# An edge-gated graph layer: another order of the first two groups, and earlier edge lists

## The chip, the core and the metric

The kernel runs on one core of a Trainium2 chip. The metric is the device time of one execution in microseconds (us). The kernel before took 1029.48 us in the median of three runs (1023.50, 1029.48 and 1036.24).

## What is computed

There are 16 graphs (batches) over the same 1024 nodes, with 256 features each. The adjacency matrix is sparse: an entry exists with a chance of about 0.8% and on the diagonal, so a node has some nine edges. The reference, cut to what matters:

```python
pre_u = einsum('bud,dk->buk', h, W1[:d]);  pre_v = einsum('bvd,dk->bvk', h, W1[d:])
hidden = relu(pre_u[:, :, None, :] + pre_v[:, None, :, :] + b1)
S   = sigmoid(einsum('buvk,ko->buvo', hidden, W2)[..., 0] + b2[0])
a_t = einsum('buv,bud->bvd', S * A, h)
m_t = einsum('uv,bud->bvd', A, h) * h
z   = beta1 * h + beta2 * (a_t @ Wa + ba) + beta3 * (m_t @ Wm + bm)
```

Taken densely, `hidden` would have 16 x 1024 x 1024 x 256 elements. Since S is multiplied by A, only the pairs with an edge count, and the kernel computes only those.

## The kernel before

**Groups, blocks, steps.** The 16 batches are four groups g of four (GB = 4). The 1024 target nodes are eight tiles vt of 128 (NT = 8). A pair (g, vt) is a block; there are 32, and `order` (lines 376 to 379) says in which order they run. A block has T = 10 steps: two halves of 64 targets, by five chunks of 128 edge slots. So a step handles up to 128 edges for four batches, and step n belongs to block n // 10.

**One step.** GpSimd (POOL) issues an indirect DMA (line 513) that fetches, for each of the 128 slots, one row of 8 KB from `table[g]` in HBM into one of eight buffers `fetched`. The row is pre_u and h of the source node for four batches. TensorE (PE) multiplies a 0/1 matrix `mark` with X, the target's pre_v with its bias (line 622), into `pc`; VectorE (DVE) adds `pc` to the row (line 652, called the add below) and takes relu and the dot product with W2 for each of four batches (line 659, the gate); ScalarE (ACT) applies the sigmoid (662) and scales the left operand (630, 666); PE sums the weighted rows h of the edges into `acc` (675). The buffer is then free, and POOL issues the fetch of step n + 8 into it.

**Once per block.** `halves` makes X of the next block from `hT`, the tile of h with the features on the partitions (pieces at the steps s = 0, 2, 5, 6, 7 of a block); `turn_over` and `block_end` transpose the sums, multiply by Wa and Wm and store z (pieces at s = 4 to 7, line 746; line 714 is VectorE's part of it).

**The tables.** `table[g]` has to stand before the first fetch of group g, eight steps ahead of that group's first block. For each of its eight tiles, `rows` computes pre_u in two halves (four matmuls by w_u on line 411 each, an ACT copy `tab`, and a DMA to the table, line 439), and `copy_h` sends h from HBM to HBM (405). `plan` (lines 806 to 814) sets the steps of the halves for groups 1 to 3. `load_hT` (400) loads the tile h that `rows` and `halves` need, in pieces of 512 bytes; a block of group 0 has it in the tile `wide` already. Places for it are few, so the tiles in `again` are dropped after their rows and loaded a second time.

**The lists.** `lists(vt)` (236 to 346) makes the edge list of one target tile for all groups: a key load from the adjacency (238), VectorE work to find and order the entries (245 to 300), three ACT operations for `mark` (305 to 307), a cast, four DMAs and five matmuls that spread it (309 to 316), and VectorE work for the row numbers `uidx` that the fetches need (323 to 344). Its values come by ten small indirect DMAs on POOL (353, `val`), one or two a step, behind a fetch. Lists 0 to 3 are made before the first step; 4 to 7 run beside the steps: `start_list` (803) names the step at which each begins. `lists` is a generator. At a yield of "op" it gives way until the next place between two gate pieces (`fill` on 658, four places a step); "load", "wait", "slot" and "step" make it pause for some steps (642).

**Queues.** Every engine runs its instructions in the order in which this code issues them. SP's queue issues nearly all plain DMAs, POOL's all indirect ones.

## Time and profile before

| | |
|---|---|
| three runs, us | 1036.24, 1029.48, 1023.50 |
| the profiled execution, us | 1026.43 |
| its span from the first to the last instruction, us | 1024.6 |
| mean granted TensorE clock | 0.984 |
| busy: PE, DVE, ACT, POOL, us | 957.0, 948.3, 889.0, 438.2 |
| moved by DMA | 375.00 MB, mean 366 GB/s |
| first add (line 652) starts at, us | 60.4 |

The profile is one execution. Where this document speaks of block k, it means the stretch from the start of the first add of block k to that of block k + 1; the windows of the trace are cut there. The windows give the busy time of each engine, the granted share of TensorE's clock (PEclk), the busy share of the 16 DMA engines and the rate. Busy minus length is idle time of that engine.

### The profile page before, as it was taken

Reading aid. Unit: us, or ns where it says so; the run is one execution under the profiler, and the core shown is the slowest. Engines: PE = TensorE matmul, PEld = TensorE weight load, DVE = VectorE, ACT = ScalarE, POOL = GpSimd, SP = SyncE. Lnnn points to the kernel's source line nnn. Section 1 sums busy time; section 2 is a strip of 40 time slices with the busy share of each in tenths; the row PEclk is TensorE's granted clock in tenths of the full one; section 3 lists DMA queues with packets and bytes.
Section 4 is the critical chain, followed back from the end, with each engine's and each line's share of the span. In section 5 each row is a group of like instructions: output and inputs, shape, how many; then the busy total and the mean of one; then the engine's idle time right before and its main releaser. Section 6 shows DMA issues by size and latency. Waiting matters only on the chain.

```text
span 1024.6 us, 21644 instructions
## 1 busy us (share of the span) xinstructions
PE 957.0 (93%) x6408; PEld 696.9 (68%) x6408; DVE 948.3 (93%) x3302; ACT 889.0 (87%) x2754; POOL 438.2 (43%) x441
## 2 busy tenths in 40 slices
PE   7877989998899999999999999999999999999996
PEld 5744766665566766776677777777777666677663
DVE  7588969879998999998999999999999999999994
ACT  3666978978898999888999999999999999999984
POOL 3166656555337332563343333434333434444430
PEclk9988999999999999999999999999999999999998
DMA  9899999999899999999999999999999999999992
GB/s 329 300 356 383 376 340 322 351 364 343 301 342 343 396 412 387 343 365 381 411 414 411 411 406 405 412 393 414 383 413 394 383 375 365 365 370 368 377 369 70
DMA packets 128702, 375.00 MB, mean 366 GB/s; under 512 B 17616, under 2 KB 83152, under 8 KB 92368
## 3 DMA queue, kind: packets, MB, share of 16 engines
q0 software_dynamic: 48640, 296.70, 74.3%
q1 hardware_dynamic: 79312, 76.30, 22.4%
q8 instruction: 53, 0.87, 0.3%
q10 hardware_dynamic: 624, 0.52, 0.2%
q14 instruction: 73, 0.60, 0.2%
HBM read 377.53 MB, written 50.33 MB: 418 GB/s over the span
## 4 chain that ended last, share of the span: by engine, by line
PE 56%; DVE 23%; ACT 8%; issue 8%; DMA 3%; POOL 1%; another core or an unknown queue 0%; POOLq 0%; DVEq 0%
PE misc L411 16%; DVE fetched L659 11%; PE misc L746 11%; PE pc L622 10%; PE acc L675 9%; DVE fetched L652 8%; PE misc L697 4%; DMA fetched<-table,uidx 3%; ACT left L666 2%; PE misc L730 1%; DVE LT L714 1%; PE misc L415 1%; ACT ev L683 1%; ACT X L906 1%; POOL fetched L513 1%
## 5 line engine op out<-in xcount | busy, mean ns | idle before, releaser
L513 POOL DMA_INDIRECT fetched<-table,uidx x320 | 342.7, 1071 | 501.3 <-PE acc L675 353.8
L659 DVE SCALAR_TENSOR_TENSOR fetched<-fetched,w_b 128x256 f32<-128x256 f32 x1280 | 472.3, 416 | 0.0
L652 DVE TENSOR_TENSOR fetched<-fetched,pc 128x1024 f32<-128x1024 f32 x320 | 387.6, 1211 | 28.9 <-PE pc L622 10.2
L666 ACT ACTIVATE left<-left,gt 128x16 f32<-128x16 f32 x1280 | 285.8, 299 | 0.0
L622 PE MATMUL pc<-X,mark 128*128 128x512 f32 x640 | 229.8, 451 | 20.7 <-DVE fetched L652 11.9
L675 PE MATMUL acc<-fetched,left 128*32 128x256 f32 x2560 | 183.6, 388 | 4.6 <-ACT ev L683 3.1
L622 PEld LDWEIGHTS pc<-X,mark 128*128 128x128 f32 x640 | 105.0, 189 | 109.8 <-issue 59.3
L675 PEld LDWEIGHTS acc<-fetched,left 128*32 128x32 f32 x2560 | 71.8, 109 | 81.9 <-issue 23.2
L662 ACT ACTIVATE gt<-sc,b_b 128x4 f32<-128x4 f32 x320 | 96.8, 303 | 30.4 <-DVE fetched L659 22.0
L746 PE MATMUL misc<-w_a,LT 128*128 128x256 f32 x496 | 117.4, 379 | 0.7 <-ACT LT L424 0.7
L746 PE MATMUL misc<-w_m,LT 128*128 128x256 f32 x496 | 117.3, 379 | 0.0
L746 PEld LDWEIGHTS misc<-w_a,LT 128*128 128x128 f32 x496 | 93.6, 189 | 15.6 <-ACT LT L424 1.5
L630 ACT ACTIVATE left<-onehot,val 128x32 f32<-128x32 bf16 x320 | 100.1, 313 | 0.0
L411 PE MATMUL misc<-w_u,wide 128*128 128x256 f32 x384 | 92.0, 388 | 8.0 <-DMA w_u<-in_W_dram 7.3
L353 POOL DMA_INDIRECT val<-in_adjT_dram,vidx x80 | 85.0, 1063 | 33.8 <-issue 22.8
L659 DVE DVE_READ_ACCUMULATOR fetched<-fetched,w_b 128x1 f32 x1280 | 99.0, 77 | 0.0
L683 ACT COPY ev<-acc 128x512 f32<-128x512 f32 x160 | 92.3, 577 | 6.8 <-PE acc L675 2.3
L746 PEld LDWEIGHTS misc<-w_m,LT 128*128 128x128 f32 x496 | 89.5, 190 | 9.8
L697 PE MATMUL misc<-ident,ev 128*128 128x128 f32 x642 | 83.9, 275 | 11.7 <-ACT ev L683 5.8
L411 PE MATMUL misc<-w_v,wide 128*128 128x256 f32 x368 | 91.5, 394 | 0.0
L697 PEld LDWEIGHTS misc<-ident,ev 128*128 128x128 f32 x642 | 74.5, 142 | 22.4 <-ACT ev L683 6.6
L411 PEld LDWEIGHTS misc<-w_u,wide 128*128 128x128 f32 x384 | 73.6, 194 | 21.1 <-DMA w_u<-in_W_dram 7.3
(160 smaller groups left out, 980.2 us busy)
## 6 DMA issues: line engine op xcount, KB each, us to landing
table<-in_x_dram SPq DMA_DIRECT2D x32, 512.0 KB
out_dram<-z SPq DMA_DIRECT2D x62, 256.0 KB
table<-tab SPq DMA_DIRECT2D x48, 256.0 KB
wide<-in_xT_dram SPq DMA_DIRECT2D x18, 512.0 KB
fetched<-table,uidx POOLq DMA_INDIRECT x320
hT<-in_xT_dram SPq DMA_DIRECT2D x10, 512.0 KB
wide<-in_xT_dram SPq DMA_DIRECT2D x4, 1024.0 KB
table<-fetched SPq DMA_DIRECT2D x8, 512.0 KB
```

The lines of the kernel that those rows point to most:

```text
L411: nc.tensor.matmul(p[:, bb * D:(bb + 1) * D], hT[:, 2 * h + bb, i, :], wt[:, i, :], start=(i == 0 and not begun), stop=(i == DC - 1), skip ...
L513: nc.gpsimd.indirect_dma_start(out=fetched[at_slot[n]], out_offset=None, in_=table[g], in_offset=bass.IndirectOffsetOnAxis(ap=uidx[:, vt * ...
L622: nc.tensor.matmul(pcs[n][:, c], marks[n // TW][:, j * P:(j + 1) * P], cuts[k][w][:, c], start=True, stop=True)
L630: nc.scalar.activation(lefts[n][:, 1::GB, :], onehot[:, vt * NW + w, j, :].unsqueeze(1).to_broadcast([P, GB // 2, V]), AF.Copy, scale=val[ ...
L652: nc.vector.tensor_tensor(t, t, pcs.pop(n), ALU.add)
L659: nc.vector.scalar_tensor_tensor(t[:, b, :], t[:, b, :], 0.0, w2_b, ALU.max, ALU.mult, accum_out=sc[:, b:b + 1])
L662: nc.scalar.activation(gt, sc, AF.Sigmoid, bias=b2_b)
L666: nc.scalar.activation(lefts[n][:, 2 * b, :], lefts[n][:, 1 + b // 2 * GB, :], AF.Copy, scale=gt[:, b:b + 1])
L675: nc.tensor.matmul(accs[i][b * 2 * V:(b + 1) * 2 * V, r, :], left[:, 2 * b - b % 2:2 * b - b % 2 + 2].rearrange("p k v -> p (k v)"), f[:, ...
L683: nc.scalar.copy(evs[i], accs.pop(i))
L697: nc.tensor.matmul(pt[:, :, FROM[j]:FROM[j] + V], evs[i][:, r, c * P:(c + 1) * P], ident, is_transpose=True, start=(j == of[0]), stop=True ...
L746: nc.tensor.matmul(pz[:, bb * D:(bb + 1) * D], LT[:, 2 * h + bb, i if bb else 1 - i, c, :], wt[:, c, :], start=(i == 1 and bb == 0 and c = ...
```

## The change

Five things change together.

1. **Order.** Group 0 runs all its eight blocks first, then group 1, 2 and 3. Before, the order was (0, tiles 0 to 5), (1, tiles 0 to 5), then tiles 6 and 7 of group 0 and of group 1. So the first block of group 1 is block 8 and not block 6, and two tiles are loaded a second time and not four; those loads are due 20 steps ahead of their block and not 9.
2. **Table 1.** Its rows are made in pairs of steps from (4, 6) to (61, 63), about one tile per block; before, from (4, 6) to (39, 41), two tiles per block.
3. **Lists.** Lists 4 to 7 start at steps 6, 12, 25 and 38, before at 7, 14, 44 and 82. They wait five steps for their key and not eight. `LISTS`, the step at which their memory goes to three more places for h, is 70 and not 110.
4. **Products.** After the three ACT operations a list now pauses two steps before its matmuls ("pause"), before one ("step").
5. **Key.** At step 0, list 4's key load is issued ahead of a load of h.

```diff
@@ lists
         nc.scalar.activation(mark, mark, AF.Relu)
-        yield "step"
+        yield "pause"
         nc.scalar.copy(few, mark)
@@ order
-    FIRST = 6
-    order = [(g, vt) for some in (range(FIRST), range(FIRST, NT)) for g in range(2) for vt in some]
-    again = [(g, vt) for g in range(2) for vt in range(FIRST, NT)]
-    order += [(g, vt) for g in range(2, NG) for vt in range(NT)]
+    TWICE = 2
+    order = [(g, vt) for g in range(NG) for vt in range(NT)]
+    again = [(1, vt) for vt in range(NT - TWICE, NT)]
@@
-    ROOM, MORE, LISTS, AHEAD = 10, 3, 110, 14
+    ROOM, MORE, LISTS, AHEAD = 10, 3, 70, 14
@@
-    turn = [(g, vt) for g in range(2) for vt in (*range(FIRST, NT), *range(FIRST))]
+    turn = [(g, vt) for g in range(2) for vt in (*range(NT - TWICE, NT), *range(NT - TWICE))]
@@ piece_of
-            r[1:] = said not in ("slot", "step"), n + {"load": 8, "wait": 2, "slot": 1, "step": 1}.get(said, 0)
+            r[1:] = (said not in ("slot", "step", "pause"),
+                     n + {"load": 5, "wait": 2, "slot": 1, "step": 1, "pause": 2}.get(said, 0))
@@
-    start_list = dict(zip((7, 14, 44, 82), range(EARLY, NT)))
+    start_list = dict(zip((6, 12, 25, 38), range(EARLY, NT)))
@@ plan
-    plan(turn[NT:], ((4, 6), (9, 11), (13, 18), (19, 21), (23, 28), (29, 31), (33, 38), (39, 41)))
+    plan(turn[NT:], ((4, 6), (9, 13), (19, 23), (29, 33), (39, 43), (49, 53), (58, 59), (61, 63)))
@@
-    pending.extend((order.index(k) * T - T + 1, k) for k in again)
+    pending.extend((order.index(k) * T - 2 * T, k) for k in again)
@@ step 0
             for i in advance[0]:
                 next(made[i], None)
+            next(made[EARLY])
             load_hT(turn[NT + 1])
-            next(made[EARLY])
```

No instruction of the list or of a block is added or removed; the program has two loads of h fewer (line 400). Three places show how the order moves. In the rows, `misc` and `pc` are accumulators, `w_u` and `w_v` the halves of W1, `hT` and `wide` the tiles of h; in the changed kernel lines 376 to about 640 have one number less.

First, TensorE at steps 40 to 43 (block 4), where `pc<-X,mark` is the product of a step. Before:

```order
L622 MATMUL pc<-X,mark 128x512 x2
L411 MATMUL misc<-w_u,wide 128x256 x4
L622 MATMUL pc<-X,mark 128x512 x2
L415 MATMUL misc<-b_p,unit 128x512
L411 MATMUL misc<-w_v,wide 128x256 x4
L675 MATMUL acc<-fetched_188,left 32x256 x4
L675 MATMUL acc<-fetched_189,left 32x256 x4
L622 MATMUL pc<-X,mark 128x512 x2
L411 MATMUL misc<-w_u,wide 128x256 x4
L622 MATMUL pc<-X,mark 128x512 x2
L415 MATMUL misc<-b_p,unit 128x512
L411 MATMUL misc<-w_v,wide 128x256 x4
```

and in the changed kernel:

```order
L621 MATMUL pc<-X,mark 128x512 x2
L410 MATMUL misc<-w_u,wide 128x256 x4
L621 MATMUL pc<-X,mark 128x512 x2
L414 MATMUL misc<-b_p,unit 128x512
L410 MATMUL misc<-w_v,wide 128x256 x4
L675 MATMUL acc<-fetched_188,left 32x256 x4
L675 MATMUL acc<-fetched_189,left 32x256 x4
L621 MATMUL pc<-X,mark 128x512 x4
L414 MATMUL misc<-b_p,unit 128x512
L410 MATMUL misc<-w_v,wide 128x256 x4
```

The second half of a table row (w_u) between the two halves of X (w_v) is gone from here.

Second, VectorE at the adds of steps 31 to 33 (block 3), where `fetched<-fetched,pc` is the add, `fetched,sc` the gate pieces and `key` and `cand` belong to a list. Before:

```order
L652 TENSOR_TENSOR fetched_189<-fetched_189,pc 128x1024
L659 SCALAR_TENSOR_TENSOR fetched_188,sc<-fetched_188,w_b 128x256 x4
L714 TENSOR_TENSOR LT<-LT,wide 128x2x4x64
L652 TENSOR_TENSOR fetched_182<-fetched_182,pc 128x1024
L659 SCALAR_TENSOR_TENSOR fetched_189,sc<-fetched_189,w_b 128x256 x4
L652 TENSOR_TENSOR fetched_183<-fetched_183,pc 128x1024
```

and in the changed kernel:

```order
L652 TENSOR_TENSOR fetched_189<-fetched_189,pc 128x1024
L245 SCALAR_TENSOR_TENSOR key<-key,ukey 128x512
L659 SCALAR_TENSOR_TENSOR fetched_188,sc<-fetched_188,w_b 128x256
L245 SCALAR_TENSOR_TENSOR key<-key,ukey 128x512
L659 SCALAR_TENSOR_TENSOR fetched_188,sc<-fetched_188,w_b 128x256 x3
L714 TENSOR_TENSOR LT<-LT,wide 128x2x4x64
L652 TENSOR_TENSOR fetched_182<-fetched_182,pc 128x1024
L254 MAX cand<-key 128x8
L659 SCALAR_TENSOR_TENSOR fetched_189,sc<-fetched_189,w_b 128x256
L254 MAX cand<-key 128x8
```

List 6 stands here now, which before was issued between steps 53 and 68; list 7, before between the adds of steps 91 and 106, is now issued between those of steps 44 and 63.

Third, SP's queue at step 0. Before:

```order
L312 DMA whose<-few 64x640 x4
L400 DMA wide<-in_xT_dram 128x8x128
L238 DMA key<-in_adjT_dram 128x1024
L96 DMA w_a<-in_Wa_dram 128x2x256
L96 DMA w_m<-in_Wm_dram 128x2x256
```

and in the changed kernel:

```order
L312 DMA whose<-few 64x640 x4
L238 DMA key<-in_adjT_dram 128x1024
L399 DMA hT_204<-in_xT_dram 128x8x128
L96 DMA w_a<-in_Wa_dram 128x2x256
L96 DMA w_m<-in_Wm_dram 128x2x256
```

List 4's key changes places with a load of h, and VectorE's first operation on it (line 245) stands one step earlier, after the add of step 7 and not of step 8.

## The prediction, as it was put on record

> **What bounds the kernel now.** I read the page's totals first, then the windows cut at each tenth add (line 652), then who waited for whom, then the chain of waits inside the longest blocks. The page:
>
> ```profile
> PE 957.0 (93%) x6408; PEld 696.9 (68%) x6408; DVE 948.3 (93%) x3302; ACT 889.0 (87%) x2754; POOL 438.2 (43%) x441
> ```
>
> PE and DVE are both busy 93% of the span, so the shares name no bound; they are an average over stages. So I cut the trace by block. Each row is one block, 0 to 12; the last two rows are blocks 13 to 22 and 23 to 30.
>
> ```profile
> 60.40:95.50 35.10, 25.12 (x125) 16.02 (x126) 28.59 (x95) 20.58 (x66) 23.01 (x22) 0.79 1.04 389
> 95.50:128.70 33.20, 32.50 (x206) 24.29 (x204) 31.34 (x122) 28.92 (x88) 21.79 (x22) 0.97 1.05 376
> 128.70:170.40 41.70, 36.49 (x222) 26.04 (x222) 33.24 (x123) 32.44 (x94) 25.93 (x25) 0.96 0.95 326
> 170.40:204.20 33.80, 31.65 (x212) 23.58 (x213) 30.20 (x111) 28.45 (x85) 19.02 (x18) 1.00 1.02 350
> 204.20:240.30 36.10, 33.52 (x220) 23.74 (x223) 28.35 (x95) 28.67 (x92) 19.98 (x20) 1.00 0.95 344
> 240.30:272.20 31.90, 27.42 (x177) 18.11 (x169) 31.59 (x114) 27.58 (x85) 11.38 (x11) 1.00 0.94 346
> 272.20:303.30 31.10, 28.68 (x209) 20.09 (x209) 29.94 (x110) 28.70 (x88) 11.46 (x10) 1.00 0.90 326
> 303.30:335.00 31.70, 29.65 (x203) 21.02 (x195) 27.92 (x94) 26.70 (x85) 22.13 (x21) 1.00 0.96 338
> 335.00:362.60 27.60, 27.39 (x178) 20.39 (x178) 27.60 (x96) 26.16 (x85) 10.73 (x10) 1.00 1.02 401
> 362.60:394.50 31.90, 30.05 (x212) 21.60 (x214) 31.90 (x120) 28.28 (x87) 10.68 (x10) 1.00 1.02 396
> 394.50:425.50 31.00, 29.66 (x190) 22.12 (x183) 29.65 (x107) 29.61 (x90) 11.35 (x11) 0.94 1.02 371
> 425.50:457.30 31.80, 30.98 (x215) 22.08 (x216) 28.15 (x94) 27.13 (x85) 21.35 (x20) 1.00 1.00 356
> 457.30:489.20 31.90, 30.06 (x208) 21.47 (x200) 27.86 (x93) 27.41 (x86) 11.89 (x12) 1.00 1.03 386
> 489.20:767.50 278.30, 277.61 (x1916) 208.89 (x1916) 277.07 (x936) 266.63 (x840) 104.13 (x99) 1.00 1.03 407
> 767.50:979.80 212.30, 206.28 (x1450) 148.79 (x1448) 211.68 (x739) 202.25 (x666) 86.39 (x80) 1.00 0.98 375
> ```
>
> The columns after the length are PE, its weight loads, DVE, ACT, POOL, then clock, DMA share, GB/s. From block 13 on DVE does not pause: 277.07 of 278.30, or 27.7 us a block, and 211.68 of 212.30 after that. There the change moves nothing. In blocks 1 to 12 DVE is idle 36.0 us (length less busy, row by row): 1.86, 8.46, 3.60, 7.75 in blocks 1 to 4; 0.31 and 1.16 in 5 and 6; 3.78 in 7; none in 8 and 9; 1.35 in 10; 3.65 and 4.04 in 11 and 12. **So the measure of this change is DVE's idle time:** DVE executes the same instructions in both kernels, and the time changes by as much as that idle time does. Blocks 9 and 10, in which list 7 runs, show what a list costs: 61.55 busy, against 55.4 for two plain blocks, 6.2 us.
>
> Who made DVE wait (all of the run):
>
> ```profile
> DVE LT L714 <- ACT LT L424: 13.8, 9, 3.3
> DVE fetched L652 <- PE pc L622: 10.2, 13, 2.4
> DVE fetched L652 <- PE acc L675: 9.9, 4, 4.9
> DVE fetched L652 <- DMA fetched<-table,uidx: 4.9, 5, 3.9
> ```
>
> Mostly PE, or ACT behind PE; a late fetch, 4.9 us in all. The chain of waits in block 4 says what PE was doing:
>
> ```profile
> 209.24 1.73 PE misc L411 x8
> ...
> 211.66 1.73 PE misc L411 x8
> ...
> 215.05 1.73 PE misc L411 x8
> ...
> 217.48 1.73 PE misc L411 x8
> ```
>
> Four half tiles of pre_u and pre_v (each eight records of 1.73 us together) within 10 us, in three steps. The ACT copies `tab` count the pre_u halves per block (the last number before the clock; blocks 1 to 5 and 7):
>
> ```profile
> 95.50:128.70 33.20, 1.78 (x3) 0.97 1.05 376
> 128.70:170.40 41.70, 2.35 (x4) 0.96 0.95 326
> 170.40:204.20 33.80, 2.33 (x4) 1.00 1.02 350
> 204.20:240.30 36.10, 1.74 (x3) 1.00 0.95 344
> 240.30:272.20 31.90, 0.00 (x0) 1.00 0.94 346
> 303.30:335.00 31.70, 1.18 (x2) 1.00 0.96 338
> ```
>
> DVE idles where there are three or four, and hardly where there are none, even beside a list.
>
> **The change part by part**, as DVE idle time taken or added.
>
> *Table 1 in pairs, one tile a block.* Blocks 1 to 5 get two halves each, as blocks 7 to 22 have, and list work in each (list 4 to 7, 6.2 us each, spread over steps 7 to 63). Idle there: 21.7 us in blocks 1 to 4. The nearest rows with a list and at most two halves are blocks 5, 9 and 10: 0.31, 0 and 1.35, mean 0.55. Four such blocks keep 2.2 us. Block 2 ran at a clock of 0.96, which is 1.7 us of PE time; I leave that in, since nothing in the edit excludes it. So 21.7 - 2.2 - 1.7 = 17.8 us go. Bounds: nothing goes, or all 21.7. The cover is DVE's own list work, which makes each step longer; if it is gone (a list that has ended), PE's 29.7 us of block 10 still lies under DVE's.
>
> *The two tiles at (58, 59) and (61, 63)* put four halves into steps 58 to 63, most in block 6. Blocks 2 and 3 had four: 8.46 and 3.60 idle, the first with a slow clock and two lists. I take block 3, so 3.6 against 1.16 now: +2.4 us. Bounds 0 and +7.3.
>
> *Lists 6 and 7 earlier.* The DVE work moves from blocks 5, 6, 9 and 10 to 3 to 6: no change of the sum. What moves with it is the values, `val` on POOL:
>
> ```profile
> 95.50:128.70 33.20, 12.14 (x12) 0.97 1.05 376
> 303.30:335.00 31.70, 10.43 (x10) 1.00 0.96 338
> 425.50:457.30 31.80, 9.85 (x9) 1.00 1.00 356
> ```
>
> Blocks 7 and 11 hold ten and nine of them and no list; beside the fetches POOL is busy 22.13 and 21.35 us there, against 10.7 in a plain block, and DVE idles 3.78 and 3.65. Block 1 has twelve beside a list and three table halves, and idles 1.86. In the changed kernel list 6's values stand beside list 7, list 7's own after it, in blocks 6 and 7. I take one of the two phases off, -3.7 us; that the values are the cause is read from where they stand, not shown. Bounds 0 and -7.4.
>
> *List 4's key ahead of h.*
>
> ```profile
> 72.12 0.53 SPq L400 DMA_DIRECT2D wide<-in_xT_dram  x1
> 72.69 2.67 SPq L238 DMA_DIRECT2D key<-in_adjT_dram  x1
> 91.74 0.69 DVE L245 SCALAR_TENSOR_TENSOR key<-key,ukey 128x512 f32<-128x512 f32 x1 [4.72 <-DMA key<-in_adjT_dram]
> ```
>
> The key took 19.0 us from issue to use, and DVE stood 4.72 us at the head of its queue. The key now goes one load earlier, but is needed a step (an add and a gate, about 2.8 us) earlier too. One load of 512 KB at block 0's 389 GB/s is 1.3 us; so I leave the wait, 0. Bounds -4.7 and +2.
>
> *The other keys* have five steps and not eight. Blocks 1 to 4 last 144.8 us, 3.6 us a step, so 18.1 us. Behind a DVE that waits for a key stand the gate, hence ACT's sigmoid, PE's sum and POOL's next fetch. The only row that shows a key late is the one above, with 19.0 us: 0.9 us each, +2 us, with shorter steps counted. Bounds 0 and +6.
>
> *SP's queue.* With a tile of table 1 move its load of h, its copy of h and its two stores, by the shapes 0.5 MB for the load, the copy and the pair of stores each. Blocks 1 to 4 make 14 halves now and 8 in the changed kernel, so three tiles, about 4.7 MB of the 50.3 MB that pass there, go to blocks 5 and 6; with each list go its key and four small stores. Fewer stores that wait for a `tab` stand ahead of the keys. DVE waited for fetches only 4.9 us in the whole run, so I take 0.
>
> *Two loads of h fewer*, 1 MB of 375: at 407 GB/s 2.6 us of transfers, beside DVE's work. 0, bound -2.6. *Products two steps behind*: PE's wait for `made` lies inside blocks that are counted already, 0. *Table 1 due at step 72*: its last rows are made at step 63, nine steps ahead; table 2 and 3 have eight (rows to 144, fetch at 152), and blocks 15 and 16 show no idle for it. 0.
>
> Block 12's 4.04 us stay: step 120 is the same in both.
>
> Sum: -17.8 + 2.4 - 3.7 + 2 = **-17 us**, so the profiled execution's 1026.4 us would be 1009.3. That execution lies 3 us under the median of the three runs, so on the median's scale it is 1012; between these I put 1010. Its own range is 997 to 1021: below, the better ends of the first and third term with the second and the keys at 0 (-29); above, a third of the first term lost and the keys at +6.
>
> **The rivals.**
>
> *Transfers bind.* If blocks 1 to 6 are slow because small loads and stores keep the DMA engines at the 338 GB/s that blocks 2 to 6 show on average, then their 71.5 MB (length by rate, row by row) take 211 us however the work is spread; they take 207.8 now. Only the values' 3.7 us and the two loads' 2.6 are gained: 1020. For it: the DMA share is 0.90 to 1.05 in every row. Against it: the share is 1.03 in blocks 13 to 22 too, at 407 GB/s, where DVE does not wait; and a late fetch cost 4.9 us in all. At 407 GB/s the 71.5 MB take 176 us, less than DVE's 190.8 us of work there (184.7 in the six rows and list 7's 6.2). The Trainium skill (DMA: Bandwidth & Descriptors, Where 436 GB/s comes from) puts the limit between HBM and one core at about 358 GB/s and the ports' at 435; by 358 those bytes would take 200 us, and the gain in blocks 1 to 6 would be 8 us, an estimate of 1015. The 407 GB/s over 278 us in the rows above is over that limit, so I go by the row.
>
> *List operations hold up the gate.* One mechanism on DVE: up to four list operations stand between the four pieces of a gate, so the sigmoid, the sum on PE and the fetch eight steps ahead all come later, and DVE then waits for what it delayed itself. If block 2's 8.46 us is its price and not that of PE's halves, blocks 1 to 5 idle 42.3 us where they now idle 22.0: +20.3 in place of -17.8, and with the other terms (+0.7) 1047. It is slower than before from 4.3 us a block on. For it: block 2 holds parts of lists 4 and 5. Against it: blocks 5 and 9 hold list work (31.59 and 31.90 busy) and idle 0.31 and 0.
>
> *Everything evens out.* If the first key comes in time and blocks 6, 7 and 11 become plain too, all idle time but block 12's and a clock window goes: 36.0 - 4.0 - 1.7 + 4.7 = 35, so 991.
>
> *The edit does not do what it says*: rows that now stand at s = 3 could collide with the next block's pieces, and the idle time of blocks 1 to 4 stays. Then only the values count: 1023.
>
> **How the numbers follow.** Forecast 0.66, of which a little over half lies below 1008.9; transfers 0.17; list operations hold up the gate 0.05; everything evens out 0.05; no effect 0.07. A measurement of this kernel tells about 2%, 20.6 us, from no change: faster than 1008.9 is 0.36 of the forecast and the 0.05, 0.41; slower than 1050.1 is the upper part of the slower rival, 0.03; 0.56 lies between. The range leaves out the slower rival and half of the fastest: 996 to 1026.
>
> **What would show it.** Right: blocks 1 to 4 at 32 to 35 us each with DVE idle under 1.5; two `tab` copies per block; blocks 8 to 11 at 28 us with no list; block 6 at 33 with PE ahead of DVE's wait. Wrong: blocks 1 to 4 still with 3 us or more of idle beside two copies (then it was not PE's halves); a rate of 340 GB/s with late fetches (transfers); a wait of several us on `key` in lists 5 to 7; POOL waiting at the first fetch of table 1.

## The result, and the profile after

The changed kernel takes 1021.1 us in the median of 19 runs, the kernel before 1028.7 us on the same chip: a ratio of 0.994, with an interval of 0.9918 to 0.9962. So it is faster by 6 us. The medians count all runs; the ratio leaves out two of the changed kernel's that fell into a slower state. The forecast was 17 us on the profiled execution; the two profiled executions differ by 5.8. Its profiled execution spans 1018.7 us, that of before 1024.6.

The page's totals show that DVE does the same work as before, as the prediction assumed; its idle time fell by 5.8 us, and so did the span.

```profile
PE 956.9 (94%) x6408; PEld 703.8 (69%) x6408; DVE 948.2 (93%) x3302; ACT 888.6 (87%) x2754; POOL 439.0 (43%) x441
```

The windows of the changed kernel, cut at each tenth add (now line 652 as before; lines 376 to 640 count one less). One row per block, 0 to 12, then blocks 13 to 22. Columns: length, PE, its weight loads, DVE, ACT, POOL, clock, DMA share, GB/s.

```profile
59.90:93.80 33.90, 25.23 (x125) 16.10 (x126) 28.90 (x95) 20.62 (x66) 23.34 (x22) 0.81 1.04 383
93.80:130.30 36.50, 32.40 (x212) 23.16 (x211) 32.55 (x122) 27.81 (x87) 26.21 (x24) 0.99 1.01 373
130.30:165.30 35.00, 31.68 (x192) 23.50 (x191) 32.52 (x124) 30.92 (x91) 20.59 (x21) 0.95 0.88 296
165.30:203.30 38.00, 34.32 (x206) 24.90 (x203) 33.52 (x128) 31.12 (x93) 23.51 (x22) 0.91 0.91 319
203.30:238.50 35.20, 32.29 (x225) 23.21 (x225) 32.61 (x121) 31.11 (x92) 19.43 (x18) 1.00 0.95 341
238.50:271.70 33.20, 29.12 (x178) 21.14 (x175) 30.05 (x114) 27.18 (x83) 21.73 (x20) 0.95 0.94 340
271.70:308.90 37.20, 36.89 (x249) 28.14 (x247) 29.45 (x101) 31.00 (x96) 17.24 (x17) 0.95 0.93 336
308.90:338.80 29.90, 28.55 (x186) 20.69 (x188) 28.04 (x95) 26.00 (x84) 15.58 (x14) 1.00 1.03 394
338.80:366.30 27.50, 27.50 (x193) 20.68 (x185) 27.50 (x96) 26.36 (x85) 10.66 (x10) 1.00 1.03 414
366.30:393.80 27.50, 27.50 (x192) 20.63 (x191) 27.50 (x94) 26.58 (x85) 10.96 (x10) 1.00 1.03 410
393.80:421.50 27.70, 27.70 (x194) 20.83 (x193) 27.70 (x96) 26.93 (x85) 10.52 (x10) 1.00 1.03 407
421.50:449.40 27.90, 27.90 (x196) 21.02 (x195) 27.72 (x94) 26.79 (x85) 10.50 (x10) 1.00 1.03 409
449.40:483.30 33.90, 31.61 (x221) 22.82 (x219) 27.95 (x97) 28.26 (x87) 11.39 (x12) 0.96 1.02 376
483.30:761.60 278.30, 278.08 (x1916) 209.45 (x1917) 277.29 (x932) 266.41 (x839) 104.97 (x100) 1.00 1.02 404
```

Blocks 8 to 11 are plain, as forecast: 27.5 to 27.9 us with DVE waiting 0.2 us at most. Blocks 1 to 4 are not: they idle 3.95, 2.48, 4.48 and 2.59 us (length less DVE), 13.5 in all, where the forecast left 3.9. Each has just two `tab` copies now, as planned (rows of blocks 1 to 4 by that tile):

```profile
93.80:130.30 36.50, 1.19 (x2) 0.99 1.01 373
130.30:165.30 35.00, 1.15 (x2) 0.95 0.88 296
165.30:203.30 38.00, 1.17 (x2) 0.91 0.91 319
203.30:238.50 35.20, 1.17 (x2) 1.00 0.95 341
```

So the idle time stayed beside two halves. The clock column shows something new: 0.95, 0.91, 0.95 and 0.95 in blocks 2, 3, 5 and 6, where the kernel before had 0.97 in block 1 and 0.96 in block 2 and 1.00 in the others. The dips come in windows of 3.41 us at half clock: five such windows begin in blocks 1 to 6, one in the kernel before. How such a stretch comes about can be read in the chain of waits at the end of block 5 (start, length, what):

```profile
265.62 0.57 ACT z L906
...
266.21 0.83 ACT made L305
...
267.07 0.83 ACT made L306
...
267.93 0.74 ACT made L307
268.67 0.20 ACT gt L662
268.87 2.10 issue
270.97 0.73 PE pc L621 x2
271.71 1.51 PE misc L315 x10
273.22 3.01 PE misc L410 x8
```

List 7's three ACT operations (2.4 us) stand ahead of the gate's sigmoid, and behind both stands a piece of X that the product `pc` of the next block needs:

```profile
269.88 1.04 ACT L906 CAST X<-low 64x1024 fp32r<-64x1024 f32 x1
```

The product starts 0.05 us after that piece. PE gets nothing to do for 2.1 us, and behind it runs eight records of a half in 3.01 us that take 1.73 at full clock. DVE then waits 4.67 us for `pc`. Two more profiles of the same kernel (again and after_timed) gave 216.1 and 214.4 us for blocks 1 to 6, against 215.1 here, with 25.5 and 24.1 us of idle time, so the stalls as a whole belong to the kernel and not to one execution. Where they fall varies: blocks 1 to 4 idle 10.9 and 11.0 us there, block 6 11.3 and 10.7.

### The profile page after: what moved, and what is told of

It is laid out like the page before. It is cut to its first block, busy times and chain, and to the rows that moved or that the text cites. A ratio compares the mean times of both kernels' runs of the same rounds, so it can differ in the third digit from the quotient of the medians.

```text
span 1018.7 us, 21649 instructions
## 1 busy us (share of the span) xinstructions
PE 956.9 (94%) x6408; PEld 703.8 (69%) x6408; DVE 948.2 (93%) x3302; ACT 888.6 (87%) x2754; POOL 439.0 (43%) x441
## 4 chain that ended last, share of the span: by engine, by line
PE 67%; DVE 16%; DMA 6%; issue 5%; ACT 5%; another core or an unknown queue 0%; SPq 0%; POOL 0%; DVEq 0%; POOLq 0%
PE misc L410 19%; PE misc L746 14%; PE pc L621 13%; PE acc L675 12%; DVE fetched L659 8%; DVE fetched L652 7%; PE misc L697 5%; DMA fetched<-table,uidx 3%; DMA hT<-in_xT_dram 2%; PE misc L730 2%; PE misc L414 1%; ACT left L666 1%; DMA wide<-in_xT_dram 1%; DVE LT L714 1%; ACT ev L683 0%
## 5 line engine op out<-in xcount | busy, mean ns | idle before, releaser
L353 POOL DMA_INDIRECT val<-in_adjT_dram,vidx x80 | 88.3, 1104 | 33.1 <-issue 22.2
L410 PE MATMUL misc<-w_u,wide 128*128 128x256 f32 x352 | 86.1, 394 | 8.4 <-DMA w_u<-in_W_dram 7.2
L410 PEld LDWEIGHTS misc<-w_u,wide 128*128 128x128 f32 x352 | 68.7, 198 | 20.9 <-DMA w_u<-in_W_dram 7.2
```

The costliest lines, as they stand in the source:

```text
L410: nc.tensor.matmul(p[:, bb * D:(bb + 1) * D], hT[:, 2 * h + bb, i, :], wt[:, i, :], start=(i == 0 and not begun), stop=(i == DC - 1), skip ...
```

## The experiments

Each kernel is the changed one with the edit shown, unless it says otherwise. The table has the ratio to the kernel before on the same chip with its interval, that kernel's median there, and from the windows of each profile the length of blocks 1 to 6, DVE's idle time in them, and the length of blocks 13 to 22. These last three columns are one execution each, in some runs a fast one for its kernel (warm 1018.9 us against a median of 1026.9, vals_twice 1029.0 against 1038.7, thin_rows 1015.2 against 1020.2). On some chips the kernel before takes 1012 us and not 1024 to 1029; ratios are set against each other only among chips of one kind.

| run | ratio [interval] | before, us | blocks 1-6 | idle | 13-22 |
|---|---|---|---|---|---|
| before | 1 | 1028.7 | 207.8 | 23.1 | 278.3 |
| changed | 0.9940 [0.9918, 0.9962] | 1028.7 | 215.1 | 24.4 | 278.3 |
| again (changed, unedited; one run) | none | 1027.9 | 216.1 | 25.5 | 283.0 |
| after_timed (changed, unedited) | 0.9950 [0.9914, 0.9986] | 1027.0 | 214.4 | 24.1 | 287.1 |
| warm | 1.0006 [0.9972, 1.0040] | 1027.9 | 216.6 | 25.0 | 278.3 |
| spread | 0.9907 [0.9877, 0.9937] | 1027.9 | 209.5 | 18.9 | 278.3 |
| no_lists | 0.9692 [0.9659, 0.9725] | 1027.9 | 182.4 | 14.3 | 278.3 |
| thin_rows | 0.9952 [0.9920, 0.9985] | 1024.3 | 209.1 | 18.3 | 278.5 |
| act_apart | 0.9881 [0.9836, 0.9926] | 1024.3 | 208.0 | 18.1 | 281.6 |
| gate_first | 0.9974 [0.9942, 1.0005] | 1024.3 | 214.9 | 19.1 | 278.4 |
| no_vals | 0.9825 [0.9792, 0.9859] | 1024.3 | 202.0 | 11.4 | 285.3 |
| before_two | 0.9922 [0.9889, 0.9955] | 1027.0 | 201.0 | 17.3 | 279.2 |
| after_two | 0.9873 [0.9824, 0.9922] | 1027.0 | 209.7 | 19.3 | 278.4 |
| all_four | 0.9875 [0.9825, 0.9925] | 1027.0 | 204.6 | 14.3 | 285.3 |
| vals_twice | 1.0263 [1.0221, 1.0306] | 1012.4 | 219.7 | 28.6 | 278.4 |
| vals_behind | 0.9908 [0.9875, 0.9941] | 1012.4 | 200.9 | 11.2 | 284.3 |
| apart_late | 0.9928 [0.9899, 0.9956] | 1012.4 | 195.6 | 5.9 | 288.8 |
| apart_late_spread | 0.9888 [0.9858, 0.9919] | 1012.4 | 194.0 | 4.3 | 288.2 |
| no_halves | 0.9952 [0.9921, 0.9983] | 1011.9 | 197.3 | 7.0 | 284.1 |
| three | 0.9918 [0.9887, 0.9950] | 1011.9 | 195.7 | 5.6 | 282.7 |

### warm: matmuls that keep the clock up

```diff
         expand(n + 2)
+        if T <= n < 7 * T and s in (0, 1, 3, 4, 9):
+            for _ in range(4 if s == 1 else 2):
+                nc.tensor.matmul(small("fill"), unit, b1_p.unsqueeze(1).to_broadcast([P, 2, D]), start=True, stop=True)
```

> The changed kernel with extra matmuls whose result nobody reads, in steps 10 to 69 at s = 0, 1, 3, 4 and 9 (two each, four at s = 1; about 2.9 us of PE per block), placed where PE waits for VectorE. Clock theory (steps that are long on VectorE leave PE idle, the granted clock halves for the window after, and PE is then late): the half-clock windows of blocks 1 to 6 go from six to at most two, VectorE idle there from 24.5 to about 16 us, and the time falls by 5 to 9 us against the changed kernel, ratio to before 0.986 to 0.990. List theory (list operations between the gate pieces hold up the chain) and cluster theory (four table halves within steps 58 to 63): the windows may go but the time stays or grows by up to 5 us, ratio 0.994 to 1.000.

The clock came back (0.99 in blocks 1 to 6, against 0.96; one window at half clock begins there), and nothing was gained: idle 25.0, the time 7 us longer than the changed kernel's. The filler itself took 28.6 us of PE there (70 records), more than the dips cost: 4% of 215 us is 8.6, an estimate. So this shows only that buying the clock with filler does not pay.

### no_lists: lists 4 to 7 copied from lists 0 to 3

```diff
     def lists(vt):
+        if vt >= EARLY:
+            yield "load"
...
+            for t in (uidx, val, onehot):
+                nc.vector.tensor_copy(t[:, to], t[:, of])
+                yield "op"
...
+            return
```

> Leaves work out: lists 4 to 7 are not made but copied from lists 0 to 3 (no key, no VectorE search, no ACT marks, no products, no value gathers), so the graph is another one; the steps, fetches and table rows are as in the changed kernel. List theory: without list operations VectorE idle in blocks 1 to 5 falls below 4 us in all, these blocks take 28 to 29 us each, and the time falls by 25 us of list work plus 12 or more of idle, ratio 0.955 to 0.960. Clock theory: much the same blocks, and the windows with PE under 0.6 busy are gone with their half clocks. Against both, if table rows or the transfers are what holds blocks 1 to 5: they stay at 31 us or more, idle time grows as list work goes, ratio 0.970 to 0.985. Block 6 stays 4 us or more over 28 by the cluster theory.

Rows of its blocks 2, 3, 4 and 6:

```profile
126.20:162.10 35.90, 31.04 (x193) 21.03 (x192) 27.87 (x94) 27.21 (x85) 25.74 (x23) 1.00 0.93 319
162.10:190.10 28.00, 27.58 (x186) 20.71 (x186) 28.00 (x102) 25.82 (x84) 10.83 (x10) 1.00 1.01 400
190.10:218.10 28.00, 28.00 (x198) 21.05 (x194) 28.00 (x102) 26.45 (x85) 10.78 (x10) 1.00 1.03 415
245.70:276.70 31.00, 31.00 (x213) 23.71 (x212) 28.00 (x95) 27.75 (x87) 9.70 (x10) 1.00 1.02 390
```

Blocks 3 and 4 hold two halves of table 1 each and DVE does not wait at all. Block 2 has no list work either, but POOL is at 25.74 us with the values of lists 0 to 3, and DVE idles 8.0 us. Block 6, with four halves and no list, idles 3.0. So with the lists their idle time goes in blocks 3 to 5, values stand beside the worst that is left, and the cluster of halves has a price of its own. Blocks 1 to 5 together keep 11.3 us, where the list theory left under 4, and the ratio missed the 0.955 to 0.960: block 12 takes 45.6 us here and idles 17.5, against 33.9 and 5.95 in the changed kernel.

### thin_rows and no_halves: less of the halves

```diff
-            half_product(p, hTs[k], w_u, h, False)
+            if tab is None and g == 1:
+                for bb in range(2):
+                    nc.tensor.matmul(p[:, bb * D:(bb + 1) * D], hTs[k][:, 2 * h + bb, 0, :], w_u[:, 0, :],
+                                     start=True, stop=True)
...
```

> The changed kernel, but each half tile of pre_u for table 1 that is made beside the steps does one of its two chunks of the product only (four records instead of eight, 0.87 us instead of 1.73); the rest of the product is left out, so table 1 holds half sums. Halves theory (the prediction's own: PE's halves of table 1 make DVE wait in blocks 1 to 6): 16 halves lose 0.87 us each, the 25 us that DVE idles in blocks 1 to 6 fall below 14, and the time falls by 10 us or more, to 1011 or less. Theories that put the wait with the lists (ACT's burst, values on POOL, list operations ahead of the gate): idle in blocks 1 to 6 stays over 19 us, the time within 6 us of the changed kernel.

The ratio is that of the changed kernel, 0.995 and 0.994. PE had half the work in these halves and the time did not move; the one profile idles 18.3, under the 19 that was named for the rivals, so a few us in a single execution may be theirs, but no gain in the median is. The test is weaker than it looks: the clock of blocks 1 to 6 fell to 0.93, so PE was busy only 7.5 us less there (189.2 against 196.7) and not the 12 that the 14 halves in these blocks would give (0.87 us each, an estimate). The other run takes the product and ACT's copy away altogether and stores a constant:

```diff
-            half_product(p, hTs[k], w_u, h, False)
...
+            if tab is None and g == 1:
+                t = w2_b.unsqueeze(1).to_broadcast([P, 2, D])
```

> The changed kernel without the products of the table-1 tiles made beside the steps and without ACT's copies of them (14 or more halves, 1.73 us of PE and 0.59 us of ACT each); their loads, copies and stores stay, but the stores write a constant, so table 1 is not computed. Halves theory in any form (PE's records or ACT's copies of table 1 make blocks 1 to 6 idle): idle there falls from 25 to under 10 us and the ratio to 0.980 or less. If the lists make these stalls by themselves: idle 15 us or more, ratio over 0.988.

Idle 7.0 and a ratio of 0.995: the one number met the theory, the other refuted it. Its blocks 3 and 4 hardly wait, with lists and values in place and no half:

```profile
156.80:191.20 34.40, 29.79 (x179) 21.39 (x171) 33.69 (x128) 30.30 (x91) 22.61 (x21) 0.90 0.99 345
191.20:223.90 32.70, 29.86 (x211) 20.32 (x211) 32.33 (x119) 30.25 (x90) 21.14 (x19) 1.00 0.97 354
```

But it ran on a chip of the faster kind, and there `three` (below) idles 5.6 with all its halves in place and is faster. How much the changed kernel idles on such a chip was not measured; vals_twice, whose edit acts only from the end of block 2 on, idles 0.00 in blocks 1 and 2 there, against 3.95 and 2.48 here. So this run neither convicts nor clears the halves, and their share of the 25 us stays open.

### act_apart: the list's ACT operations in three steps

```diff
         nc.scalar.activation(mark, slot, AF.Abs, bias=span[:, 1:2])
+        yield "slot"
         nc.scalar.activation(mark, mark, AF.Sign, bias=span[:, 0:1], scale=-1.0)
+        yield "slot"
         nc.scalar.activation(mark, mark, AF.Relu)
```

> The changed kernel with the three ScalarE operations that make a list's marks (Abs, Sign, Relu, 2.4 us back to back) in three steps instead of one. Burst theory (they stand ahead of the gate's sigmoid and left products, PE then waits for ACT, DVE for PE): four lists, up to 1.6 us less hold each and what follows of it; block 6 (list 7's burst meets the four halves) falls from 37 to about 34 us, idle in blocks 1 to 6 from 25 to about 17, the time to about 1013. Rivals (halves, values, gate): no change of block 6, the time within 3 us.

Six us faster than the changed kernel (0.9881 against 0.9940, intervals that just overlap), the size that was expected, but not in the place: block 6 kept 36.0 us and 6.5 of idle. The clock of blocks 1 to 6 rose to 0.99 with no filler, and no window at half clock begins in them:

```profile
92.30:300.30 208.00, 191.56 (x1248) 137.76 (x1247) 189.94 (x700) 178.07 (x534) 128.23 (x119) 0.99 0.98 351
```

That the three operations make the dips is not shown by this: after_two and all_four (below) have the same edit and keep three and four such windows. By the Trainium skill (TensorE: Matmul & The Clock Gate, Part 1: The HAM clock gate) the clock halves after an idle window of about 3.4 us. Here it fell without one: in the changed kernel PE was busy 1.2 to 2.0 us of the 3.41 ahead of each dip, with no gap longer than 2.3 us.

### gate_first: list operations behind the gate

```diff
         for b in range(GB):
-            fill(n)
             nc.vector.scalar_tensor_tensor(t[:, b, :], t[:, b, :], 0.0, w2_b,
                                            ALU.max, ALU.mult, accum_out=sc[:, b:b + 1])
+        for b in range(GB):
+            fill(n)
```

> The changed kernel with the same four list operations per step, but behind the four pieces of the gate instead of between them. Gate theory (list operations between the pieces delay the sigmoid, then PE's sum, then the fetch): the sigmoid of a step with list work comes 1 to 2 us earlier, idle in blocks 1 to 6 falls from 25 to under 12 us, the time to 1010 or less. Rivals (halves, burst, values): the same work in front of the next add, idle stays over 19 us, the time within 4 us.

DVE idles 5.3 us less and is busy 5.1 us more (195.8 against 190.7), so blocks 1 to 6 last as long as before: 214.9. The rival of the prediction in which list operations hold up the gate falls as the main cause: with the sigmoid ahead of them DVE still idles 19.1 us, where that theory left under 12, and nothing is gained.

### no_vals, vals_twice, vals_behind: the value gathers

```diff
-        wanted.extend((i, j) for i in range(vt * NW, (vt + 1) * NW) for j in range(TW))
+        if vt < EARLY:
+            wanted.extend((i, j) for i in range(vt * NW, (vt + 1) * NW) for j in range(TW))
+        else:
+            nc.vector.tensor_copy(val[:, sl], val[:, (vt - EARLY) * NW:(vt - EARLY + 1) * NW])
```

> The changed kernel, but the values of lists 4 to 7 are copied from those of lists 0 to 3 by one DVE operation each and not gathered by POOL: 64 indirect transfers fewer, the list work otherwise as it was (the output holds wrong values there). Values theory (the small gathers on POOL's queue hold up the fetches in blocks 1 to 7): blocks 3 to 7 fall by 2 to 4 us each, the time by 10 us or more. Rivals (halves, burst, gate): blocks with a list still idle 2 to 7 us, the time within 5 us.

The number in this text is off: 40 gathers were left out, not 64. The output holds other lists' values there. The time fell by 12 us against the changed kernel (0.9825 against 0.9940, intervals apart). Rows of blocks 3 to 6:

```profile
161.00:194.50 33.50, 30.26 (x210) 22.29 (x208) 33.50 (x127) 31.18 (x93) 10.70 (x10) 1.00 0.94 349
194.50:227.40 32.90, 31.73 (x227) 23.25 (x227) 32.53 (x120) 31.16 (x93) 11.15 (x11) 1.00 0.98 367
227.40:259.50 32.10, 28.72 (x175) 20.88 (x173) 29.95 (x115) 26.77 (x82) 10.13 (x10) 0.95 0.94 351
259.50:292.50 33.00, 32.74 (x222) 25.08 (x221) 29.41 (x103) 29.64 (x93) 9.69 (x10) 1.00 0.94 347
```

The list work is there (127 and 120 DVE instructions in blocks 3 and 4), so are two halves, and DVE waits 0 and 0.4 us; in the changed kernel it waits 4.5 and 2.6. In blocks 3 to 6, from which the gathers are gone, it waits 6.1 us in all, against 18.0 to 22.5 in the three profiles of the changed kernel; in blocks 1 and 2, whose gathers belong to lists 0 to 3 and stay, 5.3 against 6.4 in the first of them. This is the plainest single result.

Doubling the same 40 gathers, into a scratch tile:

```diff
+            if i >= EARLY * NW:
+                nc.gpsimd.indirect_dma_start(
+                    out=again_val[:, i, j:j + 1], out_offset=None, in_=adj_flat,
...
```

> The changed kernel, but each of the 40 value gathers of lists 4 to 7 is issued a second time into a scratch tile: 40 more small gathers on POOL's queue, nothing else. Leaving these 40 out gained 12 us. Values theory (each gather costs the loop some 0.3 us): 8 to 15 us slower than the changed kernel, 1029 to 1036. Clock theory (the gain without them came from other phases of the same stalls, fewer half-clock windows): within 5 us of the changed kernel, whatever the sign.

It is 26 us slower than the kernel before; the values theory had named at most 15 more than the changed kernel. POOL is busy 32.66 of 42.10 us in block 3, and the fetches themselves come late (first its window, then DVE's waits from 155 to 240 us: total, times, longest):

```profile
155.10:197.20 42.10, 36.05 (x217) 26.04 (x210) 33.89 (x127) 33.20 (x100) 32.66 (x31) 0.85 0.82 270
```

```profile
DVE fetched L658 <- DMA fetched<-table,uidx: 13.7, 9, 3.2
```

In the changed kernel itself DVE shows no wait for a row in blocks 1 to 6 (one wait of 2.7 us has a cause that the profile does not tell): by the semaphore events of the trace the rows land 2 to 9 us ahead of their add in blocks 2 to 5 and 0.4 to 9 in block 6. So vals_twice slows the loop by another path. What carries the cost of the gathers in the changed kernel is not settled; that leaving them out takes it away is shown by no_vals. A part of that gain may be the clock's: two windows at half clock begin in blocks 1 to 6 there, and not five.

In vals_behind all gathers stay, but go behind the pair of fetches:

```diff
         refill()
-        fetch_val(1 + (n % 3 == 0))
...
         while done < min(last_in, total):
             gather_in(done)
             done += 1
+        for n in range(begun, done):
+            fetch_val(1 + (n % 3 == 0))
```

> The changed kernel, but where two steps are aggregated in a pair, POOL issues both fetches first and the two to three value gathers behind them, instead of between them. Values theory with the second fetch as its path (it is issued 1.3 to 2.6 us late, so its rows come late): 5 us or more faster. Rival (the rows land 3 to 10 us ahead of the add in these blocks, so the delay is covered): within 3 us of the changed kernel.

A ratio of 0.9908 on a chip of the other kind, where the changed kernel was not measured: by itself inconclusive.

### spread: no four halves within six steps

```diff
-... (39, 43), (49, 53), (58, 59), (61, 63) ...
+... (39, 41), (43, 49), (51, 53), (59, 63) ...
```

> The changed kernel with table 1's last rows at other steps: (39, 41), (43, 49), (51, 53), (59, 63) in place of (39, 43), (49, 53), (58, 59), (61, 63). No more than three halves fall into a block and none in neighbouring steps beyond 58. Cluster theory: block 6's VectorE idle falls from 7.7 to about 3 us, blocks 4 and 5 gain under 1 us of idle, time -3 to -5 us, ratio to before 0.989 to 0.991. Clock theory: block 6 falls only if its half-clock window at 272 us goes too; otherwise it stays above 6 us and the ratio at 0.993 to 0.996.

3.4 us faster than the changed kernel (0.9907 against 0.9940, intervals that overlap), idle 18.9 against 24.4 in blocks 1 to 6, of which block 6 gave 2 (5.8, where the cluster theory left 3) and block 3, whose halves stay where they were, 2.7. So the size came near the cluster theory's, but not in its place.

### apart_late and apart_late_spread: POOL's reduction moved

```diff
-        if n == 120:
+        if n == total - 8:
             nc.vector.tensor_tensor(rest, rest, taken, ALU.subtract)
             nc.gpsimd.partition_all_reduce(longest, rest, P, bass_isa.ReduceOp.max)
-            after(n + 12, count_rest)
+            after(n + 7, count_rest)
```

Both also have act_apart's edit, and apart_late_spread has spread's.

> The changed kernel with the list's three ScalarE operations in three steps (as in the run that spread them alone) and the POOL reduction of step 120 moved to step 312, behind the last fetch. Block 12 holds 4 to 6 us of DVE idle in every kernel and 17 in one. If POOL's reduction (10 us of silence on POOL, two fetches behind it) is its cause, block 12 becomes plain (27.8 us, idle under 0.5) and the time is 4 to 6 us below the spread operations alone, 1007; the tail gets at most 1 us. If not, block 12 stays at 33 and the time at 1012.

> The same, and the last four tiles of table 1 at steps (39, 41), (43, 49), (51, 53) and (59, 63), so that no six steps hold four halves. Cluster theory (the four halves at 58 to 63 cost block 6 its 6.5 us): another 3 to 4 us, 1003 to 1004. Rival (the cluster and the list's ScalarE operations were one stall, gone already): no difference from the run beside it.

Block 12 did become plain, 28.0 and 27.9 us, instead of 33.6 in vals_twice on the same chip. But blocks 13 to 22 took 288.8 and 288.2 us, against 278.4 there, so in these executions nothing was left. With the rows spread as well the median is 3.8 us lower (1005.5 to 1001.7) and block 6 takes 31.5 and not 33.5, the size that the cluster theory named; the intervals overlap. The timeline of apart_late shows where the growth lies (start, length, engine; in brackets the idle time before and its releaser):

```profile
482.11 8.33 SPq L440 DMA_DIRECT2D table<-tab  x1
...
490.54 1.88 SPq L401 DMA_DIRECT2D wide<-in_xT_dram  x1
...
492.08 3.75 PE L412 MATMUL misc<-w_u,wide 128*128 128x256 f32 x8 [7.04 <-DMA wide<-in_xT_dram]
...
496.57 1.22 DVE L654 TENSOR_TENSOR fetched<-fetched,pc 128x1024 f32<-128x1024 f32 x1 [8.28 <-PE pc L623]
```

SP needs 8.33 us to issue one store, the load of h behind it comes late, and PE and DVE wait. In the plain blocks the DMA engines are full (share 1.02 to 1.03) and SP's queue falls behind; that the stall of block 12 had given it time to catch up is a reading and not shown. Against it stand runs with the reduction where it was, in which blocks 13 to 22 grew too (no_vals, vals_behind, no_halves, three, again: 282.7 to 285.3). The Trainium skill (DMA: Bandwidth & Descriptors, Queues, rings and completion order) says that each DMA engine takes turns between the queues packet by packet; that fits a queue of small packets that starves beside fetches of 8 KB, but no run here isolates it. In those five runs the longest wait is another one, of 3.9 to 6.3 us for the row of the first add of table 2. This is its line in `three`:

```profile
548.42 1.22 DVE L654 TENSOR_TENSOR fetched<-fetched,pc 128x1024 f32<-128x1024 f32 x1 [4.22 <-DMA fetched<-table,uidx]
```

after_timed, with 287.1 us, has a wait of 6.1 us for `pc` in these blocks.

### before_two, after_two, after_timed: the two list edits with and without the change

Both have act_apart's and vals_behind's edits, on the kernel before and on the changed one.

> The kernel before, without the change, but with its lists' three ScalarE operations in three steps and POOL's value gathers behind the pair of fetches. If these two, and not PE's three or four halves per block, made DVE idle in blocks 1 to 4, that idle time falls from 21.7 to under 12 us with the halves where they were, and the time by 8 us or more (ratio 0.992 or less). Halves theory (the prediction's term): blocks 1 to 4 keep 17 us or more, the ratio stays over 0.996.

> The changed kernel with the same two edits. If the two made both kernels' stalls, and the change moved lists and values without mending them, it gains as much here as in the kernel before, and the two differ by 6 us or less, as they do without the edits; blocks 1 to 6 idle under 12 us instead of 25. If the change's own gain was hidden by these stalls, the difference grows to 12 us or more.

> The changed kernel itself, timed on the same chip as the three runs beside it, since the kernel before differs by 1.2% between chips: ratio to the kernel before 0.994 as in its own measurement, within 0.003.

In the kernel before, with all its halves where they were, the two edits take the idle time of blocks 1 to 4 from 21.7 to 13.2 us and 8 us off the time (1027.0 to 1019.1). That is nearer the first theory, though it missed its 12. In the changed kernel they take 8 us too (0.9950 to 0.9873, intervals that just overlap), but only 5 us of idle time: blocks 1 to 6 keep 19.3, of which 8.2 in block 6, where the expectation was under 12. The change is worth 5 to 6 us without the edits and about 5 with them (0.9922 and 0.9873, intervals that overlap).

### all_four and three: the edits together

> The changed kernel with the list's ScalarE operations in three steps, the value gathers behind the pair of fetches, the last four tiles of table 1 spread, and POOL's reduction at step 312. If the edits act on different stalls they add: blocks 1 to 6 idle under 5 us, block 12 at 28 us, ratio 0.980 or less. If they shorten the same stalls: ratio 0.985 to 0.989, as with three of them (0.9888).

> The changed kernel with the list's ScalarE operations apart, the value gathers behind the pair of fetches and the rows spread, and POOL's reduction left at step 120. If the reduction only shares a stall that comes anyway (SP's queue is behind in the plain blocks), this is as fast as with it moved: ratio 0.984 to 0.988, block 12 at 33 to 36 us. If the moved reduction gained on its own: ratio 0.990 or more.

all_four comes to 0.9875, as expected if the edits shorten the same stalls, and the same as with the two list edits alone: block 12 went from 35.7 to 27.9 us and blocks 13 to 22 from 278.4 to 285.3. In these two executions the gain of block 12 is given back almost whole. three missed its 0.984 to 0.988 (0.9918, on a chip of the other kind, which is what the other theory named); its block 12 is at 34.6 as expected, and beside apart_late_spread (0.9888) the intervals overlap, so whether the moved reduction is worth something is unclear. The fastest that compute the whole result and were measured beside both kernels are these two list edits, alone or with the rest: after_two takes 1015.5 us and all_four 1015.0, where the changed kernel takes 1020.8 and the kernel before 1027.0.

## Why the prediction was half right

By the prediction's terms, as idle time of DVE against the profile before (length less busy of the rows above and of the prediction's; the last column has the two further executions, again and after_timed):

| term | forecast | measured | two more |
|---|---|---|---|
| blocks 1 to 4, table 1 in pairs | -17.8 | -8.2 | -10.7, -10.7 |
| four halves at 58 to 63, block 6 | +2.4 | +6.6 | +10.2, +9.5 |
| block 5 | none | +2.8 | +2.9, +2.1 |
| values, blocks 7 and 11 | -3.7 | -5.4 | -6.6, -7.1 |
| block 10, list 7 gone | none | -1.4 | -1.4, -1.2 |
| first key, block 0 | 0 | -1.5 | +1.2, -2.5 |
| the other keys | +2 | 0 | 0, 0 |
| block 12 | 0 | +1.9 | +1.7, +2.2 |
| sum | -17 | -5 | -3, -8 |

**Right:** that DVE's idle time is the measure; that blocks 8 to 11 become plain; that the idle time beside the values of blocks 7 and 11 goes, more of it than the half that was taken; that list work between the gate pieces is not what mainly holds the kernel up. The keys were priced too high: list 4's, whose wait of 4.72 us the sum had kept, cost none any more, and the others, at 2 us, cost none either. The line shows no wait for a key of lists 4 to 7 in this execution; `fetched` stands for keys of lists 0 to 3 (idle before line 245, by what ended it):

```profile
its engine sat idle before it (us, times) until:
  DMA fetched<-in_adjT_dram: 1.9, 1
  issue: 0.5, 1
```

Of the 4.7 us block 0 gained 1.5, and between -1.2 and 2.5 in the two further executions: the adds waited instead.

**The step that failed** is the first term: "The nearest rows with a list and at most two halves are blocks 5, 9 and 10 ... mean 0.55. Four such blocks keep 2.2 us." They kept 13.5 (10.9 and 11.0 in the two further executions). Those three blocks differ from blocks 1 to 4 in two things at least and not one: they have fewer halves, and they have no value gathers but one. It stands in the prediction's own rows: POOL is busy 11.4, 10.7 and 11.4 us there, and 19.0 to 25.9 in blocks 1 to 4. Block 1, with three halves and 1.86 us of idle time, and blocks 7 and 11, with two halves, no list and 3.78 and 3.65, spoke against the count of halves too. The idle time was put to the halves; no_vals, with list and halves left in place, made blocks 3 and 4 idle 0 and 0.4, and thin_rows, with the halves halved and the values left, gained nothing in time. The values had been priced only in blocks 7 and 11, where they stand alone.

What is shown is that two halves do not make such a block plain, and that leaving out the gathers takes most of the idle time of the blocks that hold them. That the halves had no share is not shown: no_halves, with all gathers in place, idles 0.7 and 0.4 us in blocks 3 and 4, on a chip where the changed kernel was not measured. And by which path the gathers make DVE wait stays open.

**From that follow the next two rows.** The change brings lists 6 and 7 from blocks 5, 6, 9 and 10 to blocks 3 to 6, beside the values of lists 4 to 6. POOL's busy time in block 5 went from 11.38 to 21.73 us, and DVE's idle time there from 0.3 to 3.2: a block of the kind that idles, made from one that did not. In block 6 the price of four halves (2.4 us on top of 1.16; 3.0 in no_lists) was sized about right; what the sum lacked was list 7 in the same steps: without the value gathers block 6 idles 3.6. The three ACT operations stand in its chain of waits, but spread out (act_apart) they left it 6.5.

**Not foreseen** were the dips of TensorE's clock, which the change multiplied: 8.6 us of PE at 0.96 over blocks 1 to 6, an estimate. Each stands behind 3.41 us in which PE had too little to do. What starves it is shown for one of them, by the chain above; spreading the ACT operations left none in act_apart and three in after_two.

The rival "transfers bind" was wrong where it stood, since the rows land ahead of their adds in blocks 2 to 6. It has something for it in a part of the run that the prediction called finished: in blocks 13 to 22 the waits for a late load or a late row cost 5 to 9 us in some runs and nothing in others.

## What to carry to other kernels

Before a stall is put to one cause by comparing blocks that have it with blocks that don't, list everything in which the rows differ, the quiet engines' columns too. An engine at 43% may still bear on the stall: leaving out 40 of POOL's small transfers took 12 us here, though no wait for them shows. And where several engines run above 90%, what is gained at one stall can be lost at a later one: look at the length of the stages behind it before the gain is counted.

## What the hardware showed that was not expected

- TensorE's clock halved for 3.41 us behind stretches of that length in which PE was busy 1.2 to 2.0 us, with gaps of at most 2.3 us: eight records of 1.73 us took 3.01. In the changed kernel it happened at the same places in two executions (at 135, 176, 248 and 272 us) and at others in the third (174, 181, 201 and 266).
- Four gate pieces back to back and four list operations behind them kept DVE busy 5.1 us longer over 60 steps than the same eight interleaved (195.8 against 190.7, and 190.4 to 190.7 in all three profiles of that order).
- A reduction over partitions that itself lasts 0.39 us kept POOL from issuing fetches from 459.4 to 470.0 us, and an add behind it waited 5.4 us; with the reduction moved, block 12 took 27.9 to 28.0 us in three runs, against 32.2 to 45.6 in the changed kernel and its other edits.
- SP took 8.33 us to issue one store of 256 KB while the DMA engines were full of fetches. Such a store alone need not stall: the changed kernel's profile has one of 11.08 us at 586.8, and DVE idles 1.0 us in all of blocks 13 to 22.
